# A convolution kernel's last wait: TensorE instead of SyncE waits for all stores and clears the semaphores

## The chip, the cores and the metric

The kernel runs on one core of a Trainium2 chip. The metric is the device time of one execution in microseconds, given as the median of several runs. Beside it there is one profiled execution, whose span runs from the first to the last instruction that the profiler recorded.

## What is computed

The input `x` has 8 images of 32 channels with 128 x 128 values, in float32. The reference normalizes it in 16 groups of two channels, convolves the result with a 3 x 3 kernel, adds a bias, and adds `x`:

```python
g = v.reshape(B_, G, C_ // G, H_, W_)               # _gn, G = 16
m = jnp.mean(g, axis=(2, 3, 4), keepdims=True)
s = jnp.var(g, axis=(2, 3, 4), keepdims=True)
normal = (g - m) / jnp.sqrt(s + 1e-5)
...
fx, wf = fft2(pad(normal, 256), "ortho"), fft2(pad(weight, 256), "ortho")
sp = ifft2(einsum("bihw,oihw->bohw", fx, wf), "ortho").real
out = sp[:, :, 64:64 + 128, 64:64 + 128] + bias     # sh = sw = (256 - 128) // 2
x = x + out
```

The transforms have 256 points a side and the cut starts at 64, so only a corner of the output holds products of the convolution; the rest of it is `x` plus the bias. Because of the orthonormal scaling the convolution carries a factor of 1 / 256, which the kernel folds into the normalization.

## The kernel before, in words

**Layout.** The host splits each image into its four row and column parities, so that one image is a tile of 128 partitions (4 parities x 32 channels) with 64 x 64 values each. Two images share an SBUF tile, `pairs[0]` to `pairs[3]`; all eight images stay in SBUF from their load to their store, and the result is written over the input.

**Order of the work.** The program is written out by hand, engine by engine, through a helper class `Queues`. A call `put(engine, emit, *needs)` emits one instruction on one engine's queue, waits for the semaphores of what it needs, and, where marked, increments a semaphore of its engine (`done_pe`, `done_dve`, `done_act`, `done_pool`). Line 87 is the helper's separate wait instruction, used where an instruction needs more than one wait. Loads each have a semaphore of their own; all stores share the semaphore `stored`, to which each adds 16 when it has landed.

**Loads** (line 175): SyncE issues nine DMAs at the start: image 0 in two halves with the weights (`wb_sb`) between them, image 1 in two halves, images 2 and 3 one each, and the last two pairs as one DMA each.

**Each image** then passes these steps: VectorE sums it (line 282) and ScalarE sums its squares (line 302); TensorE adds these up over the partitions of a group (`group`, line 317); ScalarE and VectorE make the mean and the deviation (lines 329 to 346); ScalarE writes the normalized corner `g` (line 360); TensorE multiplies it in three chunks of rows with four weight matrices each (`multiply`, line 399); VectorE adds the products and the bias to `x` (`add`, line 415); GpSimd adds the bias to the part of the image that has no products (`add_bias`, line 381). TensorE's instructions for the images are kept back and emitted as a hardware loop of four rounds (`emit_loop`; the loop is at line 133, its register additions at line 138).

**Stores** (line 423): SyncE issues seven DMAs. Pairs 0 and 1 go out whole, images 4, 5 and 6 one by one, and image 7 in two parts: first its lower rows, which need only GpSimd, then its upper rows, which need VectorE's two last adds. Seven stores make `stored` reach 7 x 16 = 112.

**The end** (lines 519 to 525). After the last store there are no more instructions on any engine but one. The program asserts that SyncE has waited, directly or through what it stored, for everything that the other engines signal. Then SyncE waits for all stores, and clears the kernel's semaphores, numbers 99 (`done_pe`) to 112 (`stored`), in one instruction:

```python
nc.sync.wait_ge(put.sems["stored"], put.done["stored"])
...
nc.sync.sem_clear(range(numbers[0], numbers[-1] + 1))
```

In the built program the wait and the clear are one instruction, which waits for `stored` to reach 112; the profile has it at line 525. The start of the program, with its own barrier over the five engines, has line 551 (the call that creates the program).

Of the kernel before, what the change touches and what calls it, by code (L numbers as in the profile page):

```python
# [147 lines left out]
def conv_preact_kernel(nc: bass.Bass, x: bass.AP, wb: bass.AP, out: bass.AP):  # L148
# [14 lines left out]
    put = Queues(nc)  # L163
# [258 lines left out]
    def store(to, of, *needs):  # L422
        return put("sp", lambda sp: sp.dma_start(to, of), *needs, adds="stored")
# [88 lines left out]
    stored = store(to[:, 0:N, :], xt[:, 0:N, :], biased[B - 1][1], *added[B - 1])  # L512
# [6 lines left out]
    for of, value in stored[0].items():  # L519
        seen[of] = max(seen.get(of, 0), value)  # L520
    assert all(seen.get(of, 0) == done for of, done in put.done.items()), (seen, put.done)
    nc.sync.wait_ge(put.sems["stored"], put.done["stored"])
    numbers = sorted(sem.num for sem in put.sems.values())
    assert numbers == list(range(numbers[0], numbers[0] + len(numbers)))
    nc.sync.sem_clear(range(numbers[0], numbers[-1] + 1))


# [34 lines left out]
```

## Time and profile before

| | |
|---|---|
| median of 12 runs | 83.69 us (83.49 to 84.21) |
| profiled execution, its time | 83.92 us |
| profiled execution, its span | 82.6 us |
| busy: PE, PEld | 67.0 us (81%), 41.6 us (50%) |
| busy: DVE, ACT, POOL | 50.2, 48.0, 30.2 us |
| moved by DMA | 33.62 MB in 2208 packets, mean 407 GB/s |
| granted TensorE clock, mean | 0.966 |
| last instruction of ACT, POOL, PE, DVE ends | 66.15, 69.25, 73.67, 75.18 us |

PE is TensorE's array, PEld its weight loads, DVE is VectorE, ACT ScalarE, POOL GpSimd and SP SyncE. A letter q behind an engine (SPq, PEq, PEldq) means its sequencer: waits, branches, DMA issues and semaphore instructions, which are not counted as busy time. `<-` after an instruction or an engine is followed by what it waited for. The page cuts the span into 40 equal slices and gives the busy share of each in tenths. In lists of one source line, three numbers with slashes are the shortest, median and longest duration in ns. The span ends with the last recorded instruction of the kernel, while the time of the execution is longer by 1.32 us; the trace also holds the events of semaphores ahead of the span and behind it.

### The profile page before, as it was taken

Reading aid. Unit: us, or ns where it says so; the run is one execution under the profiler, and the core shown is the slowest. Engines: PE = TensorE matmul, PEld = TensorE weight load, DVE = VectorE, ACT = ScalarE, POOL = GpSimd, SP = SyncE. Lnnn points to the kernel's source line nnn. Section 1 sums busy time; section 2 is a strip of 40 time slices with the busy share of each in tenths; the row PEclk is TensorE's granted clock in tenths of the full one; section 3 lists DMA queues with packets and bytes.
Section 4 is the critical chain, followed back from the end, with each engine's and each line's share of the span. In section 5 each row is a group of like instructions: output and inputs, shape, how many; then the busy total and the mean of one; then the engine's idle time right before and its main releaser. Section 6 shows DMA issues by size and latency. Waiting matters only on the chain.

```text
span 82.6 us, 684 instructions
## 1 busy us (share of the span) xinstructions
PE 67.0 (81%) x222; PEld 41.6 (50%) x222; DVE 50.2 (61%) x43; ACT 48.0 (58%) x55; POOL 30.2 (37%) x41
## 2 busy tenths in 40 slices
PE   0009979999999999999999999999999999960000
PEld 0005445666666666666666666666666566620000
DVE  0019836973996799499769949995995260034000
ACT  6107957992996699389669947974994700000000
POOL 6809500000069900119966800940490095000000
PEclk9999999999999999999999999999999999999655
DMA  2899999999969989997959979989979999999993
GB/s 44 317 404 413 428 421 440 452 413 428 555 302 492 492 349 428 508 444 317 508 254 508 460 333 476 508 365 397 508 333 421 444 421 444 428 421 408 423 430 143
DMA packets 2208, 33.62 MB, mean 407 GB/s; under 512 B 256, under 2 KB 288, under 8 KB 416
## 3 DMA queue, kind: packets, MB, share of 16 engines
q1 hardware_dynamic: 2208, 33.62, 96.7%
HBM read 16.84 MB, written 16.78 MB: 407 GB/s over the span
## 4 chain that ended last, share of the span: by engine, by line
PE 77%; DMA 6%; ACT 5%; DVE 2%; issue 0%
PE ps L399 71%; DMA x<-x_dram 6%; ACT unused L302 5%; PE ps L433 2%; PE ps_m L317 2%; DVE x L415 2%; PE ps_w L257 1%; ACT origin L291 0%
## 5 line engine op out<-in xcount | busy, mean ns | idle before, releaser
L399 PE MATMUL ps<-g,w_sb 128*128 128x363 f32 (+1 forms) x192 | 59.9, 468 | 0.0
L399 PEld LDWEIGHTS ps<-g,w_sb 128*128 128x128 f32 x192 | 35.6, 192 | 19.5 <-ACT origin L291 1.6
L282 DVE TENSOR_REDUCE sums<-x 128x1 f32<-128x4096 f32 x7 | 30.9, 4411 | 0.6 <-DMA x<-x_dram 0.6
L302 ACT ACTIVATE unused<-x,origin 128x4096 f32<-128x4096 f32 (+1 forms) x9 | 30.0, 3331 | 0.3
L381 POOL TENSOR_SCALAR x<-x,bias_sb 128x1984 f32<-128x1984 f32 (+3 forms) x12 | 23.2, 1945 | 17.1 <-ACT origin L291 12.8
L415 DVE SCALAR_TENSOR_TENSOR x<-ps,bias_sb,x 128x1089 f32<-128x1089 f32 (+2 forms) x9 | 10.9, 1221 | 7.6 <-PE ps L399 7.6
L360 ACT ACTIVATE g<-x,rstd 128x1089 f32<-128x1089 f32 (+2 forms) x9 | 10.7, 1201 | 3.9 <-DVE rstd L346 3.9
L282 DVE TENSOR_REDUCE first_sums<-x 128x1 f32<-128x2048 f32 x2 | 4.6, 2288 | 6.3 <-DMA x<-x_dram 6.3
L250 POOL COPY sums<-x 128x1 f32<-128x1 f32 x6 | 1.0, 183 | 18.6 <-DMA x<-x_dram 18.6
L334 DVE TENSOR_SCALAR var<-ps_m,square 128x1 f32<-128x1 f32 x8 | 1.7, 218 | 7.2 <-ACT square L329 7.2
L257 PE MATMUL ps_w<-x,avg 128*128 128x1 f32 x4 | 1.0, 314 | 6.0 <-DMA x<-x_dram 6.0
L329 ACT ACTIVATE square<-ps_m,origin 128x1 f32<-128x1 f32 x8 | 2.1, 262 | 6.5 <-PE ps_m L317 6.5
L433 PE MATMUL ps<-x,avg 128*128 128x512 f32 x6 | 5.8, 1108 | 0.0
L257 PEld LDWEIGHTS ps_w<-x,avg 128*128 128x128 f32 x4 | 1.2, 323 | 7.0 <-issue 7.0
L317 PEld LDWEIGHTS ps_m<-sums,avg 128*128 128x128 f32 x16 | 2.7, 188 | 2.3 <-DVE x L415 1.0
L340 ACT ACTIVATE std<-var,eps 128x1 f32<-128x1 f32 x8 | 2.4, 295 | 2.3 <-DVE var L334 2.3
L343 DVE RECIPROCAL rstd<-std 128x1 f32<-128x1 f32 x8 | 1.3, 164 | 2.9 <-ACT std L340 2.9
L291 ACT ACTIVATE origin<-ps_w 128x1 f32<-128x1 f32 x2 | 0.3, 160 | 4.3 <-PE ps_w L257 4.3
L462 POOL COPY w_sb<-wb_sb 32x128 f32<-32x128 f32 (+1 forms) x8 | 2.5, 339 | 0.0
L317 PE MATMUL ps_m<-sums,avg 128*128 128x3 f32 x16 | 2.4, 218 | 0.0
L433 PEld LDWEIGHTS ps<-x,avg 128*128 128x128 f32 x6 | 1.8, 334 | 1.0 <-issue 1.0
L317 PEld LDWEIGHTS ps_m<-first_sums,avg 128*128 128x128 f32 x4 | 1.2, 324 | 1.7 <-ACT unused L302 1.2
(19 smaller groups left out, 11.4 us busy)
## 6 DMA issues: line engine op xcount, KB each, us to landing
x<-x_dram SPq DMA_DIRECT2D x2, 4096.0 KB, 33.5
out_dram<-x SPq DMA_DIRECT2D x2, 4096.0 KB, 16.9
out_dram<-x SPq DMA_DIRECT2D x3, 2048.0 KB, 9.9
x<-x_dram SPq DMA_DIRECT2D x4, 1024.0 KB, 7.9
x<-x_dram SPq DMA_DIRECT2D x2, 2048.0 KB, 17.4
out_dram<-x SPq DMA_DIRECT2D x1, 1056.0 KB, 7.3
out_dram<-x SPq DMA_DIRECT2D x1, 992.0 KB, 11.8
wb_sb<-wb_dram SPq DMA_DIRECT2D x1, 62.0 KB, 5.0
```

The costliest lines, as they stand in the source:

```text
L257: "pe", lambda e: e.matmul(ps_w[:, img : img + 1], avg, xts[img][:, 0, 0:1], start=True, stop=True),
L282: lambda e: e.tensor_reduce(to_sum(img, k)[:, 0:1], piece, mybir.AxisListType.X, ALU.add),
L302: lambda e: e.activation(unused[:, rows.start * W : rows.stop * W], piece, AF.Square, bias=origins[img], accum_out=to_sum(img, k)[:, 1:2],),
L317: lambda e: e.matmul(ps_ms[:, 0 : of.shape[1]], avg, of, start=(part == 0), stop=(part == last)),
L329: lambda e: e.activation(squares[img], ps_ms[:, 0:1], AF.Square, bias=origins[img]),
L340: lambda e: e.activation(stds[img], variances[img], AF.Sqrt, bias=eps, scale=float(FFT * FFT)),
L360: lambda e: e.activation(g[:, rows, :], xt[:, LO + rows.start : LO + rows.stop, LO:W], AF.Identity, bias=rstd[:, 1:2], scale=rstd[:, 0:1],),
L381: put("pool", lambda e: e.tensor_scalar(part, part, 1.0, bias_sb, op0=ALU.mult, op1=ALU.add), *free, mark=mark)
L399: lambda e, k=k, dc=dc, rows=rows, top=top: e.matmul(ps[:, 0:rows, 0 : N - dc], w_sb[:, k * P : (k + 1) * P], g[:, top : top + rows, dc:N] ...
L415: lambda e: e.scalar_tensor_tensor(part, in0=ps, scalar=bias_sb, in1=part, op0=ALU.add, op1=ALU.add),
L433: "pe", lambda e: e.matmul(pss[1][:, 0, :], avg, piece, start=True, stop=True),
L462: lambda e: e.tensor_copy(w5[to, :, dc, :, c.start * C : c.stop * C], taps[:, 1 - rin : 5 - rin, b, :].rearrange("p (dr r) b o -> p dr r ( ...
```

## The change

One engine's name changes in two lines. The wait for `stored` and the clear move from the end of SyncE's instructions to the end of TensorE's, behind its loop. All other instructions stay as they were, on the same engines, in the same order: TensorE gets one instruction more, and SyncE has one less.

```diff
@@ -519,10 +519,10 @@
     for of, value in stored[0].items():
         seen[of] = max(seen.get(of, 0), value)
     assert all(seen.get(of, 0) == done for of, done in put.done.items()), (seen, put.done)
-    nc.sync.wait_ge(put.sems["stored"], put.done["stored"])
+    nc.tensor.wait_ge(put.sems["stored"], put.done["stored"])
     numbers = sorted(sem.num for sem in put.sems.values())
     assert numbers == list(range(numbers[0], numbers[0] + len(numbers)))
-    nc.sync.sem_clear(range(numbers[0], numbers[-1] + 1))
+    nc.tensor.sem_clear(range(numbers[0], numbers[-1] + 1))
```

## The prediction, made before the changed kernel was run

> **What bounds the kernel now.** I read the page first, its slices above all.
>
> ```profile
> span 82.6 us, 684 instructions
> ...
> PE   0009979999999999999999999999999999960000
> ...
> DMA  2899999999969989997959979989979999999993
> ...
> q1 hardware_dynamic: 2208, 33.62, 96.7%
> ```
>
> A slice is 82.6 / 40 = 2.07 us. PE ends four slices before the end, while the DMA row stays at 9 until the last one, and the queue's packets fill 96.7% of the span. So the end is set by the last store's landing. The chain of waits gives PE 77%, but its list in order of time stops with DVE:
>
> ```profile
> 73.70 1.48 DVE x L415 x2
> ```
>
> That is 75.18 us. The 7.4 us from there to 82.6 us stand in no row of the chain; they are the drain of the final stores, as SyncE's own waits show, with the instruction that the change moves:
>
> ```profile
> SPq L525 <- DMA out_dram<-x: 7.0, 1, 7.0
> ```
>
> and that line of the kernel by itself:
>
> ```profile
> L525 SPq EVENT_SEMAPHORE_RANGE_CLEAR  x1: 55/55/55, 82.5 to 82.5; - x1
> ```
>
> The timeline has nothing on any compute engine behind the two DVE adds, and SyncE's last issue before the clear is at 75.21 us (332 ns). By the windows view the DMA share is 0.86 from 75.5 to 82.1 us, and 0.00 from 82.1 to 82.6 us: the last half microsecond is completion and one instruction.
>
> The clear itself, from the records behind these views: the sixteenth increment of `stored` came at 82.529 us, the clear started at 82.545 (16 ns later), ended at 82.600, and had zeroed the 14 semaphores from 82.559 to 82.579. It is the span's last instruction. So everything from 82.529 us on is on the path, whichever engine does it, and nothing before is touched: the matmuls, adds, queues and stores are the same instructions in the same order on all five engines, with one instruction taken from SyncE's end and put at TensorE's end.
>
> **What comes after the span.** The time of this execution is 83.92 us, 1.32 us more than its span. The trace has the events of a semaphore number 2, which the kernel does not allocate (its own are 99 to 112). They come in groups of nine (us from the span's start):
>
> ```
> before the kernel:  -0.371 -0.336 -0.298 -0.254 -0.231 | -0.120 -0.081 -0.047 -0.001
> after it, first:    73.838 73.872 73.910 75.326 82.714 | 82.759 82.797 82.831 82.879
> after it, second:   83.671 83.775 83.814 83.858 83.881 | 83.979 84.018 84.052 84.099
> ```
>
> I read nine events of five engines as a barrier that runs as a chain: five arrivals in a fixed order, then four steps back. The first group after the kernel tells the order. ACT's last instruction ended at 66.15 us and POOL's at 69.25, yet the first arrival is at 73.838, 158 ns after TensorE's last matmul signalled (73.680), and two more follow within 72 ns: **TensorE is first in the chain**, and the two idle engines could only follow it. The fourth comes 132 ns after DVE's last add signalled (75.194): VectorE. The fifth comes 114 ns after SyncE's clear: **SyncE is last**. Behind this barrier the trace has all semaphores being zeroed (82.835 to 83.447 us), then the second group.
>
> The Trainium skill describes such a thing: "Runtime: NRT & Kernel Launch", section "The ~15µs preamble/postamble breakdown", has a serpentine over five engines at 44 ns a hop, eight hops, at both ends of a kernel. It names no order. "Trainium Architecture — The Big Picture", section "Naming decoder ring", numbers TensorE 0 and SyncE 4, which is the order found above. By the page's hop, four more hops would cost 176 ns as an estimate, where the rows below give 206.
>
> **The change, part by part.** All sums are on the profiled execution (83.92 us, 0.23 above the median of the 12 runs, 83.69, and within their 83.49 to 84.21); what comes out is a difference, added to either.
>
> 1. *SyncE loses the wait and the clear.* After its issue at 75.21 us it has nothing left, goes into the barrier early, and waits there in place of line 525. No other instruction or DMA of SyncE stands behind the clear. Gain taken: the 16 + 55 ns, and the 114 ns to its arrival, all given to TensorE in the next steps.
>
> 2. *TensorE wakes.* Behind the clear on TensorE's queue there is no work of the kernel, only its own arrival. TensorE's wait instructions start 28 or 29 ns after the releasing event where they really waited (5.923, 8.244, 10.925, 18.806 us); SyncE's 16 or 17. Added: 28 - 16 = **12 ns**.
>
> 3. *TensorE clears.* A range clear on TensorE is not in the trace. The nearest rows are the two engines' waits at line 551:
>
> ```profile
> L551 SPq EVENT_SEMAPHORE  x1: 17/17/17, 0.7 to 0.7; - x1
> ...
> L551 PEldq EVENT_SEMAPHORE  x1: 51/51/51, 0.7 to 0.7; - x1
> ```
>
> The first fence line is the same 17 ns as in all seven waits of SyncE, and 51 ns is the time of all twelve of TensorE. Lower end: 0, the clear is one request and DRAIN takes 7 ns on SyncE and 8 on TensorE. Upper end: the ratio 51 / 17 = 3 on the whole clear, 55 x 3 = 165, so 110 more. Taken: the fixed difference, 51 - 17 = **34 ns**, since the nearest row shows one sequencer step. All twelve rows were at a granted clock of 1.0, and the windows view has 0.50 at the end, where TensorE has long been idle; doubling the clear for that, 55 + 34 more, stays within the 110.
>
> 4. *TensorE leaves the kernel.* From its last signal to its arrival took 158 ns (73.680 to 73.838); SyncE needed 82.714 - 82.579 = 135 from its clear's last write, VectorE 132. Added: 158 - 135 = **23 ns**; the ends are 0 and 23, since part of the 158 can be the array's emptying.
>
> 5. *The chain.* With SyncE late, four arrivals were already in: from its arrival to the last step back took 82.879 - 82.714 = 165 ns. With TensorE late nobody has arrived: its arrival must pass ACT, POOL, DVE and SyncE, then come back. The group before the kernel shows this, none waiting long: -0.371 to -0.001 = 370 ns. Added: 370 - 165 = **205 ns**. It splits into 140 for the four steps forward (35 + 38 + 44 + 23) and 66 for the first step back, 111 instead of 45, as VectorE has only just passed the arrival on (rounding makes it 206). The second group after the kernel agrees: 83.775 to 84.099 = 324, plus a first step of 35, is 359 (its own 104 is long for ACT's late zeroing). Ends: 140, if the step back stays short, and 205.
>
> Sum: 12 + 34 + 23 + 205 = **274 ns slower**. Ends: 12 + 0 + 0 + 140 = 152, and 12 + 110 + 23 + 205 = 350. Nothing covers it: the whole core is idle there, and the zeroing and the second group follow the barrier's last step, which frees TensorE: the long part of the zeroing, semaphores 7 to 53, runs from 83.099 to 83.447, 220 ns after that step, and ends last.
>
> "Trainium Architecture — The Big Picture", in its table of engines, gives SyncE to barriers and semaphore plumbing and TensorE to matmul; that speaks against the change without a price, and the 17 against 51 ns above is what the trace has of it.
>
> **Forecast:** 83.92 + 0.27 = 84.19 for an execution like the profiled one; 83.69 + 0.27 = 83.96 in the median, 0.33% slower. Anything within 0.2% (0.17 us) is about what a measurement of this kernel cannot tell from no change.
>
> **Rivals.**
>
> *The reported time stops before the barrier* (no change). Then only steps 2 and 3 count, 12 to 122 ns: 83.70 to 83.81. Decides if each engine's end is stamped as it leaves the kernel. For it: 1.32 us outside the span can lie wholly ahead. Against: it would then begin at -1.32 us, where none of the trace's events lies (semaphore 2 is silent from -2.420 to -0.371); beginning at the group's last step (-0.001) it ends at 83.92, inside the second group, which is behind the moved part.
>
> *TensorE stumbles on its way out.* Its last branch was at 68.713 us, so whatever its sequencer does between loop and barrier had 5 us of cover under the last matmuls until 73.68; now it can stand in the open. SyncE and VectorE leave in 114 to 135 ns without such cover, which speaks against it. The nearest price: the loop's taken branches lasted 207 to 225 ns, the last one 76, so a jump costs some 150: 83.96 + 0.15 = 84.11, and 84.15 with the upper end of step 3.
>
> *The chain runs otherwise and TensorE is its cheap end* (faster): then the 140 ns of steps forward would have been paid before and are saved, and with the 66 of the step back, less 46 for steps 2 and 3: 83.69 - 0.16 = 83.53. Decides if the arrivals at 73.84 us were not TensorE's. Against: no event of semaphore 2 lies between -0.001 and 73.838, though two engines were idle from 66 and 69 us.
>
> **Numbers.** Forecast 0.71, stop before the barrier 0.15, stumble 0.08, other order 0.06. The forecast's own ends are 83.69 + 0.15 and + 0.35: 83.84 to 84.04. The range reaches up to the stumble's 84.15 and down to 83.76, half into the first rival, for a median that itself moves. Of the forecast, some 0.05 falls within 0.2% at its low end. Slower by over 0.2%: 0.66 + 0.08 = 0.74; within: 0.15 + 0.05 = 0.20; faster: 0.06.
>
> **What the changed profile would show.** The span ends with the clear on TensorE's sequencer, 28 ns after the last landing, lasting about 89 ns: span near 82.65, with no other row moved. SyncE's wait at line 525 is gone from its list. In semaphore 2's first group after the kernel no event lies before the clear, and all nine lie within some 370 ns behind it; the second group comes as much later. The prediction is wrong if those nine events come spread as before, if the clear lasts much over 165 ns, if TensorE arrives long after it, or if the events move and the reported time does not.

## The result, and the profile after

The changed kernel takes 84.05 us in the median of 13 runs (83.87 to 84.35), the kernel before 83.64 us in its 52 runs by now. The ratio is 1.0044, 95% interval 1.0029 to 1.0059: slower by 0.37 us (0.0044 x 83.64), between 0.24 and 0.49. The forecast was 0.27 us, 83.96 in the median: the right way and inside the stated range (83.76 to 84.15), but too small by some 0.1 us. The measured median lies just above the forecast's own ends (83.84 to 84.04).

The profiled execution took 83.95 us, nearly that of before (83.92). That is no contradiction: its last store happened to land earlier, at 82.162 us instead of 82.529, so 83.95 - 82.162 = 1.79 us lie behind the landing, where 83.92 - 82.529 = 1.39 us did. The difference, 0.40 us, is inside the interval of the ratio. All readings from here on start at the last landing, since what lies ahead of it varies by several tenths of a microsecond from one execution to the next. Three of the experiments below, e1, e3 and e5, were profiled in executions that were some 2% slower as a whole than the fastest of the same kernel, and only this stretch of theirs is read.

The page of the changed kernel, its first line, slices and queue:

```profile
span 82.3 us, 684 instructions
...
PE   0019965999999999999999999999999999990000
...
DMA  2899999999979979989959989989979999999994
...
q1 hardware_dynamic: 2208, 33.62, 96.8%
```

The same shape: TensorE's array done four slices ahead of the end, the DMA engines at work into the last slice. The list of SyncE's own waits has lost its line 525, and the wait at the program's start is all that remains below the stores:

```profile
SPq L423 <- DVE x L415: 34.8, 6, 6.9
SPq L87 <- POOL x L381: 32.2, 2, 23.7
SPq L551 <- PEq L551: 0.7, 1, 0.7
```

Line 525 by itself now stands on TensorE's sequencer:

```profile
L525 PEldq EVENT_SEMAPHORE_RANGE_CLEAR  x1: 152/152/152, 82.2 to 82.2; - x1
```

It takes 152 ns where SyncE's took 55. Behind the span, semaphore 2 has these events, in us from the span's start:

```
ahead of the kernel:  -0.370 -0.336 -0.298 -0.254 -0.231 | -0.119 -0.080 -0.046  0.001
behind it, first:     82.535 82.569 82.607 82.651 82.675 | 82.772 82.811 82.846 82.893
behind it, second:    83.680 83.808 83.846 83.891 83.914 | 84.012 84.051 84.085 84.131
```

No arrival is early any more. Before, four of the nine stood ahead of the clear, at 73.84 to 75.33 us; now all nine stand behind it. From the last landing on, the two executions compare so (ns):

```
                                            before   after   more   forecast
wake: last landing to the clear's start         16      29     13         12
clear                                           55     152     97         34
leaving: clear's end to arrival                114     192     78         23
chain: arrival to the ninth event              165     358    193        205
sum, last landing to the ninth event           350     731    381        274
ninth event to the end of the second group    1220    1238     18          -
tail: last landing to the second group's end  1570    1969    399
```

The forecast column's two middle rows are its 34 for the clear and its 23 for leaving. The reported time is 1.041 us behind the ninth event before and 1.057 after; in the experiments' profiles it is 1.027 to 1.061, all but one (e11: 1.386, where two events ahead of the kernel are missing as well; not explained). Its distance to the span's end goes from 1.30 to 1.86 us in the same profiles. So the reported time follows the ninth event, and not the span: the time does not stop ahead of the barrier.

### The profile page after: what moved, and what is told of

Read it like the earlier page. It is cut to its first block, busy times and chain, and to the rows that moved or that the text cites. A ratio compares the mean times of both kernels' runs of the same rounds, so it can differ in the third digit from the quotient of the medians.

```text
span 82.3 us, 684 instructions
## 1 busy us (share of the span) xinstructions
PE 66.3 (81%) x222; PEld 41.2 (50%) x222; DVE 50.2 (61%) x43; ACT 48.0 (58%) x55; POOL 30.2 (37%) x41
## 4 chain that ended last, share of the span: by engine, by line
PE 75%; ACT 7%; DMA 6%; DVE 3%; issue 1%
PE ps L399 72%; DMA x<-x_dram 6%; ACT unused L302 5%; DVE x L415 2%; PE ps_m L317 2%; ACT g L360 1%; PE ps_w L257 1%; ACT std L340 0%; ACT square L329 0%; DVE rstd L346 0%; DVE var L334 0%; ACT origin L291 0%; DVE rstd L343 0%
## 5 line engine op out<-in xcount | busy, mean ns | idle before, releaser
L399 PE MATMUL ps<-g,w_sb 128*128 128x363 f32 (+1 forms) x192 | 60.6, 472 | 1.1 <-ACT g L360 1.1
L433 PE MATMUL ps<-x,avg 128*128 128x512 f32 x6 | 4.8, 935 | 0.0
L346 DVE TENSOR_SCALAR rstd<-ps_m,rstd 128x1 f32<-128x1 f32 x8 | 1.8, 219 | 0.3
```

The costliest lines, as they stand in the source:

```text
L399: lambda e, k=k, dc=dc, rows=rows, top=top: e.matmul(ps[:, 0:rows, 0 : N - dc], w_sb[:, k * P : (k + 1) * P], g[:, top : top + rows, dc:N] ...
L433: "pe", lambda e: e.matmul(pss[1][:, 0, :], avg, piece, start=True, stop=True),
```

## The experiments

Three questions were open. Is the chain's 193 ns a matter of TensorE's place in it, or of its speed? Why are the clear and the way out so much longer than forecast? And does the loop's end or the halved clock play into that? Ratios of these runs are to the kernel before on the same chip; runs on those chips spread more widely (the kernel before from 83.49 to 85.66 us), and most intervals are half a per cent to each side. So the verdicts rest on the trace, whose stretches repeat within 10 ns in kernels that end alike. The table has them in ns (last op: the clear, or the wait where nobody clears; leaving, chain and tail as in the table above, the tail reaching to the end of the second group; early: arrivals that stand ahead of the clear or wait):

```
                          wake   last op   leaving   chain   early   tail
before   SyncE              16        55       114     165       4   1570
after    TensorE            29       152       192     358       0   1969
e1  ScalarE ends            21        94       114     324       1   1693
e2  GpSimd ends             24       114       533     286       2   2191
e3  VectorE ends            28       128       140     242       3   1776
e4  TensorE, no loop        29       152       191     358       0   1966
e5  TensorE, no clear       28        51       187     357       0   1864
e6  SyncE, no clear         16        17       111     165       4   1528
e7  TensorE, clears 1       28        63       192     355       0   1872
e8  TensorE, clock at 1     29       152       197     358       0   1973
e9  TensorE late, not last  86        52       120     165       4   1642
e10 TensorE, clears 4       28        65       192     359       0   1885
e11 TensorE, clears 5       28        86       193     355       0   1896
```

**e1, e2, e3: another engine ends the kernel.** The wait and the clear go to ScalarE, GpSimd or VectorE:

```diff
-    nc.sync.wait_ge(put.sems["stored"], put.done["stored"])
+    nc.scalar.wait_ge(put.sems["stored"], put.done["stored"])     # e1; e2 nc.gpsimd, e3 nc.vector
...
-    nc.sync.sem_clear(range(numbers[0], numbers[-1] + 1))
+    nc.scalar.sem_clear(range(numbers[0], numbers[-1] + 1))       # e1; e2 nc.gpsimd, e3 nc.vector
```

> ScalarE waits for the stores and clears. The tail is the time from the last store's landing to the last event of semaphore 2: 1.570 us with SyncE, 1.969 with TensorE. Theory PLACE (what counts is how far from its end the late engine stands in the chain TensorE, ScalarE, GpSimd, VectorE, SyncE, and besides, TensorE's sequencer is slow): ScalarE arrives second, so its arrival to the ninth event lasts 335 ns, as in the group before the kernel (-0.336 to -0.001), against 165 with SyncE and 358 with TensorE; wake, clear and leaving cost as with SyncE, 16 to 20, 55 and some 115 ns. Tail 1.74 us, time 0.17 us above the kernel before, ratio 1.002. Theory SPEED (the chain is long only because TensorE is slow at it): arrival to ninth event 165 ns, tail 1.57 us, ratio 1.000. In the events PLACE shows one arrival early (TensorE, 0.16 us after its last matmul) and eight behind the clear.

> GpSimd waits for the stores and clears. PLACE: third in the chain, arrival to ninth event 297 ns (-0.298 to -0.001 in the group before the kernel); two arrivals early, seven events behind the clear. Wake 24 ns and a wait of 17 ns as its rows show, so a clear of some 55; its way out is unknown, 115 ns if like SyncE's, up to 300 if its drain of 186 ns at the start comes in. Tail 1.71 to 1.90 us, ratio 1.0017 to 1.004. SPEED: arrival to ninth event 165 ns, tail 1.57 to 1.76.

> VectorE waits for the stores and clears. PLACE: fourth in the chain, arrival to ninth event 253 ns (-0.254 to -0.001 in the group before the kernel); three arrivals early, six events behind the clear. Wake about 20 to 28 ns, clear 55 to 70 (its waits take 21 ns against 17), leaving 132. Tail 1.68 to 1.71 us, ratio 1.0013 to 1.0017. SPEED: arrival to ninth event 165 ns, tail 1.59 to 1.62.

The events of the first group behind the kernel, in us:

```
e1   76.303 | 84.218 84.256 84.300 84.324 84.421 84.460 84.495 84.542
e2   75.196 75.230 | 83.784 83.828 83.851 83.949 83.987 84.023 84.070
e3   76.155 76.189 76.228 | 84.000 84.023 84.121 84.159 84.195 84.242
```

The bar is where the clear stood. One, two and three arrivals are early: the late engine is second, third and fourth, as read from the profile of before. The chain takes 324, 286 and 242 ns, each 11 ns under the expectation (335, 297, 253), mostly because the first step back took 97 or 98 ns and not the 111 of the group ahead of the kernel. SPEED, with 165 for all three, falls. Line 525 of each (e1, e2, e3, one fence for each kernel):

```profile
L525 ACTq EVENT_SEMAPHORE_RANGE_CLEAR  x1: 94/94/94, 84.0 to 84.0; - x1
```

```profile
L525 POOLq EVENT_SEMAPHORE_RANGE_CLEAR  x1: 114/114/114, 83.1 to 83.1; - x1
```

```profile
L525 DVEq EVENT_SEMAPHORE_RANGE_CLEAR  x1: 128/128/128, 83.7 to 83.7; - x1
```

The expectation of some 55 to 70 ns for the clear was wrong on all three, though their single waits take 17 to 21 ns in the median, much like SyncE's 17. In the kernel before:

```profile
L87 POOLq EVENT_SEMAPHORE  x6: 17/17/43, 18.5 to 66.1; - x6
L87 SPq EVENT_SEMAPHORE  x6: 17/17/17, 29.1 to 69.3; - x6
...
L87 DVEq EVENT_SEMAPHORE  x1: 21/21/21, 12.7 to 12.7; - x1
L87 ACTq EVENT_SEMAPHORE  x1: 17/17/17, 14.6 to 14.6; - x1
```

What a wait takes does not tell what a clear takes. In the times, e1 had a ratio of 1.0018 (0.9975 to 1.0061) and e3 1.0000 (0.9953 to 1.0047), which settle nothing; e2 had 1.0102 (1.0054 to 1.0150), slower, and its profile has where some of it comes from: GpSimd needs 533 ns from its clear to its arrival, more than the 115 to 300 expected.

**e4: no loop ahead of the clear.** TensorE's instructions are emitted as they come:

```diff
-        put.kept = []
+        pass
...
-    put.emit_loop(NPAIR, {"act": 2 * 5, "dve": 2 * 5, "pool": 2 * 2})
```

> As the changed kernel, but TensorE's instructions for the images stand written out instead of in a loop of four rounds, so that no branch lies ahead of the clear. Theory BRANCH (the 192 ns between TensorE's clear and its arrival, and the 152 ns of its clear, come from leaving the loop, code fetched late): clear and leaving fall towards SyncE's 55 and 114, the tail towards 1.80 us. Theory SEQUENCER (TensorE does such instructions slowly wherever they stand): clear 152, leaving 192, chain 358 and tail 1.97 us stay within 10 ns or so. What the loop is worth in the stages before is not the question; some change of the span is possible.

```profile
L524 PEldq EVENT_SEMAPHORE_RANGE_CLEAR  x1: 152/152/152, 83.3 to 83.3; - x1
```

The clear (at line 524 here) takes the same 152 ns, leaving 191, the tail 1.966 us. BRANCH falls. The whole kernel was slower than before by 1.0161 (1.0100 to 1.0222), more than the tail explains; its last store landed at 83.28 us, so the rest is ahead of the landing, and was not followed up.

**e5, e6: nobody clears.** The clear is left out; only the wait is left, on TensorE in e5 and on SyncE in e6:

```diff
-    nc.tensor.sem_clear(range(numbers[0], numbers[-1] + 1))      # e5, from the changed kernel
...
-    nc.sync.sem_clear(range(numbers[0], numbers[-1] + 1))        # e6, from the kernel before
```

> TensorE waits for all stores, and nobody clears the semaphores (the clear is left out; the outputs do not depend on it). If the clear's 152 ns on TensorE are its own work, the last instruction becomes a wait of 51 ns as in TensorE's other rows, and the tail falls by 0.10 us from 1.969 to 1.87; wake 29, chain 358 stay, leaving 192 or back to 158. If the 152 ns are the price of whatever TensorE does last after a long idle time, the wait takes far more than 51 ns and the tail stays at 1.97. Ratio to the kernel before: 1.0036 in the first case, 1.0048 in the second.

> SyncE waits for all stores as in the kernel before, and nobody clears (the clear is left out). The wait takes 17 ns where the clear took 55: tail 1.53 us against 1.570, 0.05% and not measurable in the time. With e5 it gives the cost of the wait's place without any clear: 0.34 us by wake 13, wait 34, leaving 40 to 80 and chain 193 plus 18 behind it. If the place mattered only through the clear, e5 and e6 would have the same tail.

The last instruction of e5, and then of e6:

```profile
L522 PEldq EVENT_SEMAPHORE  x1: 51/51/51, 83.8 to 83.8; - x1
```

```profile
L522 SPq EVENT_SEMAPHORE  x1: 17/17/17, 82.5 to 82.5; - x1
```

A bare wait is 51 ns on TensorE and 17 on SyncE, as in their other rows, and the tails are 1.864 and 1.528 us, as expected. Between these two no clear is in play: 336 ns are the price of the wait's place alone (12 wake, 34 wait, 76 leaving, 192 chain, 22 behind it). The clear adds (152 - 51) - (55 - 17) = 63 ns to that, and 336 + 63 = 399. The times settle nothing: 1.0022 (0.9977 to 1.0068) and 1.0003 (0.9955 to 1.0051). e6 has the shortest tail of all, by 42 ns against the kernel before, 0.05%, which no timing here can show.

**e7, e10, e11: TensorE clears one, four or five semaphores,** the last ones, and leaves the others as they are:

```diff
-    nc.tensor.sem_clear(range(numbers[0], numbers[-1] + 1))
+    nc.tensor.sem_clear(range(numbers[-1], numbers[-1] + 1))      # e7; e10 numbers[-4], e11 numbers[-5]
```

> TensorE waits and clears one semaphore, the stores', instead of 14 (the others are left as they are). On TensorE the 14 were zeroed from 82.220 to 82.311 us, 7 ns each, on SyncE in 20 ns, 1.5 each. If TensorE's clear costs by the semaphore, it falls from 152 to about 152 - 13 x 7 = 61 ns and the tail to 1.88 us. If it is one fixed cost, it stays near 152 and the tail at 1.97.

> TensorE waits and clears four semaphores (the last four; the others are left as they are). In the changed kernel's trace the 14 were zeroed in groups of four, 30 ns from group to group on TensorE (6.5 on SyncE); one semaphore took 63 ns in all, 14 took 152. If a group is one step, four cost as one: 63 to 70 ns, tail 1.87 to 1.88 us. If each semaphore costs (152 - 63) / 13 = 6.8 ns, four take 84 ns, tail 1.89 us.

> TensorE waits and clears five semaphores (the last five; the others are left as they are). By groups of four this is two steps: 63 + 30 = 93 to 97 ns, tail 1.90 us. By the semaphore it is 63 + 4 x 6.8 = 90 ns, 6.8 more than four.

Line 525 of e7, e10 and e11:

```profile
L525 PEldq EVENT_SEMAPHORE_RANGE_CLEAR  x1: 63/63/63, 82.7 to 82.7; - x1
```

```profile
L525 PEldq EVENT_SEMAPHORE_RANGE_CLEAR  x1: 65/65/65, 82.1 to 82.1; - x1
```

```profile
L525 PEldq EVENT_SEMAPHORE_RANGE_CLEAR  x1: 86/86/86, 82.3 to 82.3; - x1
```

Four cost as one (63 and 65 ns), and the fifth brings 21 more. e7 alone also fitted a cost by the semaphore (61 ns expected); e10 tells the two apart, with 65 ns where that cost would have made 84. So the clear goes by groups of four, not by the semaphore. The 14 of the changed kernel are four groups, and the moments at which each was zeroed show the step (ns from the clear's start; first and last of each group):

```
            99-102    103-106   107-110   111-112   step from group to group
SyncE       14, 18    20, 24    27, 31    34, 34    6 to 7
ScalarE     17, 21    35, 39    52, 56    70, 70    17 or 18
GpSimd      21, 25    43, 47    64, 68    86, 87    21 or 22
VectorE     21, 26    46, 50    70, 74    93, 95    23 to 25
TensorE     29, 33    59, 63    89, 93    119, 120  30
```

Of the 97 ns that the clear takes longer on TensorE, the three steps between four groups are 3 x 30 - (34 - 14) = 70; the other 27 lie ahead of the first group and behind the last (152 - 90 = 62 against 55 - 20 = 35), close to the 34 by which a bare wait is longer. e11's 86 ns lie 7 below the expectation by groups (93 to 97), and below the one by the semaphore (90) too, so its total does not decide. Its moments do: the first four semaphores were zeroed 25 to 31 ns after the clear's start and the fifth at 55, so the step from group to group is 30 here too, and what is shorter is the way to the first group (25 instead of 29) and the second group with its one semaphore. In the times e7 had a ratio of 1.0038 (0.9983 to 1.0093), which settles nothing; e10 and e11 ran once each (83.75 and 84.29 us).

**e8: TensorE's clock held up.** Behind the loop TensorE goes on with matmuls of 512 columns into an unused bank, until the stores have nearly landed:

```diff
+    for _ in range(9):
+        nc.tensor.matmul(ps_w, avg, w_sb, start=True, stop=True)
     nc.tensor.wait_ge(put.sems["stored"], put.done["stored"])
```

> As the changed kernel, with nine matmuls of 512 columns into an unused bank behind TensorE's loop, so that its granted clock, 0.5 at the end since TensorE went idle, stays at 1.0 until the clear. They take about 0.85 us each, 73.7 to some 81.4 us, beside the stores' drain. Theory CLOCK (the clear and the way out are slow because TensorE's clock has been halved): the clear falls from 152 to 76 ns or so, leaving from 192 towards 96 to 158, tail 1.80 to 1.86 us. Theory SEQUENCER (its sequencer is slow at any granted clock): 152, 192 and a tail of 1.97 us stay.

The clock's row in the page of the changed kernel, then that of e8, and the line of the clear in e8:

```profile
PEclk9999997599999999999999999999999999999955
```

```profile
PEclk9999998589999999999999999999999999999999
```

```profile
L527 PEldq EVENT_SEMAPHORE_RANGE_CLEAR  x1: 152/152/152, 83.3 to 83.3; - x1
```

The granted clock is 0.5 in the last two slices of the one and full to the end of the other, and the clear takes 152 ns in both, leaving 192 and 197. CLOCK falls: TensorE's sequencer takes its time at either clock. The whole kernel was at 1.0177 (1.0122 to 1.0233); again the last landing (83.31 us) is later. Some of that was there before the added matmuls began: in this profile the second half of image 0 landed at 9.11 us, against 8.41 in the changed kernel's, and the last store was issued at 76.16 us, against 75.52. The rest was not followed up.

**e9: TensorE late, but not last.** SyncE waits and clears as in the kernel before. The last store but one gets its own semaphore, `low`; TensorE waits for it with a small matmul, and SyncE waits for that too:

```diff
-    store(to[:, N:H, :], xt[:, N:H, :], biased[B - 1][0])
+    put.semaphore("low")
+    low = put("sp", lambda sp: sp.dma_start(to[:, N:H, :], xt[:, N:H, :]), biased[B - 1][0], adds="low")
...
+    op = nc.tensor.matmul(ps_w[:, 0:1], avg, avg[:, 0:1], start=True, stop=True)
+    op.wait_op(put.sems["low"], LANDED, "sem-ge")
+    op.then_inc(put.sems["pe"], 1)
+    nc.sync.wait_ge(put.sems["low"], LANDED)
+    nc.sync.wait_ge(put.sems["pe"], put.done["pe"] + 1)
     nc.sync.wait_ge(put.sems["stored"], put.done["stored"])
```

> SyncE waits for all stores and clears, as in the kernel before, and TensorE is made late too, but not last: behind its loop it waits for the last store but one (which gets a semaphore of its own) with a matmul of one column, whose end SyncE waits for ahead of its last wait. The last store but one landed at 80.01 us in the profile before, the last at 82.53. Theory PLACE OF THE LAST (only the engine that arrives last counts): TensorE's arrival moves from 73.84 to 80.3 to 81.0 us, ScalarE, GpSimd and VectorE follow it within 0.14 us, four arrivals stand ahead of the clear, arrival to ninth event stays 165 ns, tail 1.570 us within 10 ns. Theory SLOW TENSORE (a wait at the end of TensorE costs by itself, since its way back through the chain is then slow): the tail rises towards 1.76 us (193 ns of chain more) though TensorE is early.

```
e9   80.560 80.595 80.633 80.677 | 82.560 82.604 82.642 82.676 82.725
```

TensorE now arrives at 80.56 us, 6.7 us later than before, the next three follow within 0.12 us, and the chain behind SyncE's arrival is 165 ns as before. That part is PLACE OF THE LAST to the nanosecond, and SLOW TENSORE falls. The tail is 1.642 us, 72 ns over the expectation: SyncE's clear started 86 ns behind the landing instead of 16, because of the edit itself. The waits were built so that the last one ahead of the clear waits for `stored` and for TensorE's matmul, starts 17 ns behind the landing and takes 28 ns,

```profile
L528 SPq EVENT_SEMAPHORE  x1: 28/28/28, 82.3 to 82.3; - x1
```

and the clear, which itself waits for `low` alone (landed at 79.76 us), follows 41 ns later as a second instruction:

```profile
L531 SPq EVENT_SEMAPHORE_RANGE_CLEAR  x1: 52/52/52, 82.4 to 82.4; - x1
```

The ratio, 0.9974 (0.9920 to 1.0028), settles nothing.

## Why the prediction was right, and where it was short

- *What bounds the kernel.* Right. Nothing ahead of the last landing is part of the change, and all of the difference lies behind it.
- *Step 1, SyncE's gain.* Right: SyncE is in the barrier early, its 185 ns of wake, clear and leaving are gone, and TensorE's stand in their place.
- *Step 2, wake.* 12 ns, measured 13.
- *Step 3, the clear.* Taken at 34 ns more, measured 97, within the upper end of 110. This is the larger of the two mis-sized terms. The choice went by the one-step wait (17 against 51 ns) as a fixed difference; the clear is not one step but one for each group of four semaphores, 30 ns on TensorE and 6 or 7 on SyncE (e7, e10, e11). The worry about the clock was needless (e8).
- *Step 4, leaving.* Taken at 23 ns more, measured 78, and above its own upper end. The 158 ns from the last matmul's signal were the wrong row. Behind a matmul it is 157 or 158 ns in every kernel where TensorE does not end, in e9 too (signal at 80.403 us, arrival at 80.560); behind an instruction of its sequencer, a wait or a clear, it is 187 to 197 ns from that instruction's end in all seven kernels in which TensorE ends. A likely reason is that the sequencer runs ahead of the array and does part of its way out under the last matmuls; that is argued, not shown. Besides, the forecast counted SyncE's 135 ns from the clear's last write; counted so, TensorE's are 224, 89 more.
- *Step 5, the chain.* Taken at 205 ns, measured 193; the first step back took 97 instead of 111 ns. The second group's first step of 104 ns was put down to a late zeroing on ScalarE, which the trace does not show: all zeroing had ended at 83.447 us, ahead of that group's first event at 83.671. Nothing in the sum rests on it. The order of the engines, read from the early arrivals in the profile of before, holds at all five places (the two kernels and e1 to e3).
- *Rivals.* The time does not stop ahead of the barrier: the reported time keeps its distance to the ninth event. The other order is excluded by e1 to e3. That TensorE stumbles on its way out is half true: it is 78 ns slower there, but not by a branch (e4). This rival's 84.15 was added up wrongly: 84.11 and the 76 ns between step 3's 34 and 110 make 84.19.
- *The range.* Partly luck. The 381 ns of the trace lie above the forecast's own upper end of 350, and the median of 84.05 us just above its 84.04; the stated range held it because it reached on to the stumble's price, a branch that e4 ruled out.

The Trainium skill, "Runtime: NRT & Kernel Launch", section "The ~15µs preamble/postamble breakdown", has some 355 ns for the whole way there and back, in its row on the barrier ahead of a kernel. Here the group ahead of the kernel took 370 to 372 ns, and the one behind it 355 to 359 with TensorE last. What decided this case is that a late engine pays only for the part of the way that is left: 165 ns for the last engine, 358 for the first.

What stays open: what GpSimd does in its 533 ns, why each engine has its own step for a clear, why TensorE's way out differs behind a matmul and behind a clear, and what made the landings of e4 and e8 later.

## What to carry to other kernels

A kernel's last wait is on the path with everything behind it, and there each engine has its own price: find out who arrives in which order at the closing barrier from the events behind the span, and let the engine that is last in that order, here SyncE, be the one that waits. The span alone does not show it: it was shorter after the change (82.3 against 82.6 us), and the kernel slower. A row for one instruction of a sequencer is no price for another that works through a list.

## What the runs showed of the hardware that was not expected

- A range clear goes by groups of four semaphores, counted from the start of the range; one or four cost nearly the same (63 and 65 ns on TensorE), 14 cost 55 ns on SyncE, 94 on ScalarE, 114 on GpSimd, 128 on VectorE and 152 on TensorE.
- GpSimd needs 533 ns from its last instruction to its arrival at the closing barrier, TensorE 187 to 197, VectorE 140, ScalarE 114 and SyncE 111 to 120.
- TensorE's sequencer took the same 152 ns for the clear at a granted clock of 0.5 and of 1.0.
